# Layer 1's q, k and v by seven products of halves, in a two-layer graph kernel

## The chip, the cores and the metric

The kernel runs on one core of one Trainium2 chip. The core has TensorE (PE, matrix products; its weight loads are shown as PEld), VectorE (DVE), ScalarE (ACT), GpSimd (POOL) and SyncE (SP, which here issues nearly all DMAs). The metric is the device time of one execution in microseconds; less is better.

## The reference

`x` has 128 graphs of 128 nodes with 512 features, in float32; `adj` is a boolean 128x128 matrix for each graph. Two residual layers follow each other. Each one normalises `x` row by row, takes the positive part `h`, and adds an attention-like mix.

```python
# layer 0, 8 heads of 64
h   = relu(layernorm(x))
m   = h @ map_w.T + map_b;   n = m / |m| per head
q   = m @ q_w.T + q_b;       k = m @ k_w.T + k_b
p   = softmax(where(adj, -1e10, q k^T / 8)) * keep
a   = (n n^T > 0.1) * p
x   = x + relu((a @ sem) @ gcn_W.T / (sum(a) + 1))      # sem = h @ gcn_map_w.T + b
# layer 1, 4 heads of 64
h   = relu(layernorm(x))
q, k, v = h @ Wq, h @ Wk, h @ Wv                         # 512 -> 256 each
x   = x + softmax(where(adj, q k^T / 8, -inf)) @ v @ Wo + bo
```

All products are float32 products. Each float32 product appears in the profile as two records on TensorE.

## The kernel before, in words

**Blocks and turns.** Two graphs (`g` = 0, 1) make one block, so there are 64 blocks of 256 nodes. All work of a block is cut into named steps, which are methods of `Block`. The order of the steps is written out by hand in the list `TURN`: an entry `(back, step, ...)` means that in turn t the step is recorded for block t - back. A loop records the list turn by turn, and the engines run their own instructions strictly in that order. So one turn holds layer 0's projections of block t, layer 0's attention of block t - 1, its mix and layer 1's q, k and v of block t - 2, layer 1's attention of block t - 3, and its mix and output projection of block t - 4. Entries with a negative `back` prepare later blocks.

**Layer 0's projections by seven products.** `h` of a block (two graphs by two halves of the features) is a 2x2 arrangement of quarters A; the weights are a 2x2 arrangement of blocks. The four output quarters are computed with seven quarter products in place of eight, the scheme of Winograd. `halves` (L360) makes four sums S1 to S4 of the quarters of `h` on GpSimd. `sums_of_weights` (L172) makes four sums of the weight blocks, once. `p(kind, i)` (L377) is product i; products 1 and 2 go to bank X, 6, 7 and 4 to bank Y, 5 and 3 to bank Z. Between them, `r`, `u` and `c` read the banks at an intermediate state and add: `r` 1 copies X with a bias after product 1 and `r` 2 is the same with another bias; `u` 1 is Y + r after product 6, `u` 2 is Y + r after product 7; `c` writes an output quarter from a bank and one of these. As the next product adds to the same bank, it has to wait for the reader. This is done for two kinds: `qk` (query and key, weights stationary, 128-column records) and `ms` (m and sem, activations stationary, 512-column records).

**Layer 1's q, k and v.** They are plain products: `qk1` (L745) makes q and k with 8 matmuls each, weights stationary and both graphs' 256 nodes moving; `v1` (L768) has 8 matmuls with activations stationary and 256 weight columns moving. `qk1_out` and `v1_out` copy the results out of PSUM on ScalarE, q with a factor of 1/8.

**PSUM and buffers.** All eight PSUM banks are one rotating pool (`mm_bank`, L60): a new bank is the one given out eight requests before, and its first product waits for that one's last reader. SBUF pools `keep1`, `keep2`, `keep3`, `keep6` and `squares` (2 buffers) rotate in the same way.

**Transpositions.** Data that must be turned is transposed in 32x32 squares on VectorE, written to DRAM in four DMAs (`put`, L207), read back in one (`get`, L217), and joined by a ScalarE copy. This is done for layer 0's h (`h0`, `h0_put`, `h0_get`, `h0_out`), for n, for the thresholded attention (`near_T`, `near_put`, `near_get`, `near_T_out`), for layer 1's h (`h1` and so on) and for its attention (`attn_T`, `attn_put`, `attn_get`). Blocks at the start and end use TensorE for some of them.

**Layer 0's end.** `mix0` (L668) multiplies the turned attention by sem, `mix0_out` (L686) scales it into `x1`, `reload` loads x again as `xr` and `residual` (L708) adds it to `x1` on GpSimd; then `stats1`, `rstd`, `norm1`, `h1` follow.

Of the kernel before, what the change touches and what calls it, by code (L numbers as in the profile page):

```python
# [8 lines left out]
F32 = mybir.dt.float32  # L9
# [6 lines left out]
P = 128  # L16
# [4 lines left out]
def kernel(  # L21
# [51 lines left out]
    w_q1 = const.tile([P, KC, INNER], F32, name="w_q1")  # L73
    w_k1 = const.tile([P, KC, INNER], F32, name="w_k1")
    w_v1 = const.tile([P, KC, INNER], F32, name="w_v1")
# [95 lines left out]

    def sums_of_weights(w):  # L172
        nc.vector.tensor_sub(w[:, T3], w[:, B22], w[:, T1])
        nc.vector.tensor_sub(w[:, T1], w[:, T1], w[:, B11])
        nc.vector.tensor_sub(w[:, T2], w[:, B22], w[:, T1])
        nc.vector.tensor_sub(w[:, T4], w[:, B21], w[:, T2])
# [48 lines left out]
    class Block:  # L225
# [17 lines left out]
        def load_x(self, tag):  # L243
            b = self.b
            t = keep1.tile([P, G, D], F32, tag=tag, name=f"{tag}_{b}")
            nc.sync.dma_start(out=t, in_=x[b * G : (b + 1) * G].rearrange("g s d -> s g d"))
            return t


        def reload(self):  # L250
            self.xr = self.load_x("xr")
# [99 lines left out]
        def h0_out(self):  # L351
            self.hT = self.joined(("hn", 0), "hT", AF.Relu)
# [4 lines left out]
        def quarters(self):  # L357
            return [[self.hT[:, g, 2 * k : 2 * k + 2, :] for k in range(2)] for g in range(G)]

        def halves(self):  # L360
            A = self.quarters()
            t = keep1.tile([P, 4, 2, S], F32, tag="halves", name=f"halves_{self.b}")
            S1, S2, S3, S4 = (t[:, i] for i in range(4))
            nc.gpsimd.tensor_tensor(S1, A[1][0], A[1][1], ALU.add)  # L364
            nc.gpsimd.tensor_tensor(S2, S1, A[0][0], ALU.subtract)
            nc.gpsimd.tensor_tensor(S3, A[0][0], A[1][0], ALU.subtract)
            nc.gpsimd.tensor_tensor(S4, A[0][1], S2, ALU.subtract)
            self.f["S"] = (S1, S2, S3, S4)
# [8 lines left out]
        def p(self, kind, i):  # L377
            A = self.quarters()
            S = self.f.get("S")
# [10 lines left out]
            if kind == "ms":  # L390
                for c in range(2):
                    nc.tensor.matmul(  # L392
                        bank,
                        lhsT=src[:, c, :],
                        rhs=w_ms[:, w, c, :],
# [6 lines left out]
            for oc in range(KC):  # L402
                for c in range(2):
                    nc.tensor.matmul(  # L404
                        bank[:, oc * P : (oc + 1) * P],
                        lhsT=w_qk[:, w, c, oc * P : (oc + 1) * P],
# [6 lines left out]
        def sums(self, nm):  # L413
            pool = keep1 if nm == "r1" else keep2
            return pool.tile([P, D], F32, tag=nm, name=f"{nm}_{self.b}_{len(self.f)}")

        def r(self, kind, i):
            if i == 1:
                self.f[kind, "r1"] = r = self.sums("r1")
                if kind == "ms":  # L420
                    nc.vector.tensor_add(r, self.f[kind, "X"], b_ms[:, 1])
                    return
                for oc in range(KC):
                    cols = slice(oc * P, (oc + 1) * P)
                    nc.scalar.activation(
                        r[:, cols], self.f[kind, "X"][:, cols], AF.Identity, bias=b_k[:, oc : oc + 1]
                    )
                return
            self.f[kind, "r2"] = r = self.sums("r2")
            if kind == "ms":  # L430
                nc.gpsimd.tensor_tensor(r, self.f[kind, "r1"], b_d, ALU.add)
            else:
                nc.gpsimd.tensor_tensor(
                    r.rearrange("p (c t) -> p c t", t=S),
                    self.f[kind, "r1"].rearrange("p (c t) -> p c t", t=S),
# [4 lines left out]
        def u(self, kind, i):  # L440
            r = self.f[kind, "r1"]
            if i == 1:
                self.f[kind, "u1"] = self.sums("u1")
                nc.vector.tensor_add(self.f[kind, "u1"], self.f[kind, "Y"], r)  # L444
            else:
                nc.vector.tensor_add(r, self.f[kind, "Y"], r)  # L446

        def c(self, kind, g, half):
            bank, other = (("X", None), ("Z", "u1"), ("Y", "r2"), ("Z", "r1"))[2 * g + half]
            bank = self.f[kind, bank]  # L450
            if kind == "ms":
                other = b_ms[:, 0] if other is None else self.f[kind, other]
                hh = H0 // 2
                nc.vector.tensor_add(  # L454
                    mss[:, :: 1 + self.b % 2, g, half * hh : (half + 1) * hh, :DK][:, :2],
                    bank.rearrange("p (k h d) -> p k h d", k=2, d=DK),
                    other.rearrange("p (k h d) -> p k h d", k=2, d=DK),
                )
                return
            nm = ("qT", "kT")[half]  # L460
            if nm not in self.f:
                self.f[nm] = keep1.tile([P, KC, T], F32, tag=nm, name=f"{nm}_{self.b}")
            out = self.f[nm][:, :, self.cols(g)]
            if other is None:
                for oc in range(KC):
                    nc.scalar.activation(
                        out[:, oc],
                        bank[:, oc * P : (oc + 1) * P],
                        AF.Identity,
                        bias=b_q[:, oc : oc + 1],  # L470
                    )
            else:
                nc.vector.tensor_add(
                    out,
                    bank.rearrange("p (c t) -> p c t", t=S),
                    self.f[kind, other].rearrange("p (c t) -> p c t", t=S),
                )
# [208 lines left out]
        def mix0_out(self, g):  # L686
# [8 lines left out]
            if "x1" not in f:  # L695
                f["x1"] = self.x1 = keep3.tile([P, G, D], F32, tag="x1", name=f"x1_{b}")
            x1 = self.x1[:, g, :]
            for i in range(2):
                nc.vector.scalar_tensor_tensor(
                    x1.rearrange("p (i h d) -> p i h d", i=2, d=DK)[:, i],  # L700
# [7 lines left out]
        def residual(self, g):  # L708
            x1 = self.x1[:, g, :]
            nc.gpsimd.tensor_add(x1, x1, self.xr[:, g, :])  # L710
# [33 lines left out]

        def qk1(self, nm, w):  # L745
            pq = mm_bank(f"p{nm}_{self.b}").rearrange("p (c t) -> p c t", t=T)
            for oc in range(IC):
                for c in range(KC):
                    nc.tensor.matmul(  # L749
                        pq[:, oc, :],  # L750
                        lhsT=w[:, c, oc * P : (oc + 1) * P],
                        rhs=self.h1T[:, :, c, :],
                        start=(c == 0),
                        stop=(c == KC - 1),
                    )
            self.f["p", nm] = pq

        def qk1_out(self, nm):
            self.f[nm] = keep1.tile([P, IC, T], F32, tag=nm, name=f"{nm}_{self.b}")
            nc.scalar.mul(self.f[nm], self.f["p", nm], SCALE if nm == "q1" else 1.0)  # L760

        def q1(self):
            self.qk1("q1", w_q1)

        def k1(self):
            self.qk1("k1", w_k1)

        def v1(self):  # L768
            pv = mm_bank(f"pv1_{self.b}").rearrange("p (g o) -> p g o", g=G)
            for g in range(G):  # L770
                for c in range(KC):
                    nc.tensor.matmul(  # L772
                        pv[:, g, :],
# [417 lines left out]
```

## Time and profile before

| what | value |
|---|---|
| median of three runs | 3073.66 us (3071.89 to 3075.13) |
| profiled execution | 3074.49 us, its span 3072.70 us |
| granted TensorE clock, mean | 0.996 |
| one turn in the middle (1498.30 to 1544.76 us) | 46.46 us |
| busy in that turn: PE, PEld, DVE, ACT, POOL | 46.46, 35.91, 33.95, 22.96, 24.54 us |
| DMA in that turn | 0.59 of 16 engines, 172 GB/s |

A page of the profile gives the busy time of each engine with its share of the span; then the chain of work that ended last, followed back from the last instruction, at each step to what released it. A timeline row has a start and a length in us, engine, line, operation, out<-in and a count; brackets hold the idle time before it and what ended it. In the chain a row has start, length, engine, tile and line. Rows of equal instructions are merged, and the length of a merged row is from the first start to the last end, so that rows that follow each other without a gap can overlap a little.

### The profile page before, as it was taken

Reading aid. Unit: us, or ns where it says so; the run is one execution under the profiler, and the core shown is the slowest. Engines: PE = TensorE matmul, PEld = TensorE weight load, DVE = VectorE, ACT = ScalarE, POOL = GpSimd, SP = SyncE. Lnnn points to the kernel's source line nnn. Section 1 sums busy time; section 2 is a strip of 40 time slices with the busy share of each in tenths; the row PEclk is TensorE's granted clock in tenths of the full one; section 3 lists DMA queues with packets and bytes.
Section 4 is the critical chain, followed back from the end, with each engine's and each line's share of the span. In section 5 each row is a group of like instructions: output and inputs, shape, how many; then the busy total and the mean of one; then the engine's idle time right before and its main releaser. Section 6 shows DMA issues by size and latency. Waiting matters only on the chain.

```text
span 3072.7 us, 62082 instructions
## 1 busy us (share of the span) xinstructions
PE 3037.7 (99%) x23024; PEld 2337.5 (76%) x23024; DVE 2177.1 (71%) x3913; ACT 1481.6 (48%) x4573; POOL 1572.8 (51%) x2183
## 2 busy tenths in 40 slices
PE   8999999999999999999999999999999999999997
PEld 5777777777777787787777777777777777777875
DVE  3677777777777777777777777777777777777763
ACT  2454554454454554544544544544544544544543
POOL 1555456455455455455455555554564564554552
PEclk9999999999999999999999999999999999999998
DMA  5346656655655555655555556566566556556541
GB/s 162 116 144 180 186 147 179 183 156 173 182 163 172 169 177 166 172 173 172 165 175 178 159 177 182 153 178 187 148 179 184 152 176 183 160 173 174 164 131 62
DMA packets 304206, 507.97 MB, mean 165 GB/s; under 512 B 49184, under 2 KB 180512, under 8 KB 295968
## 3 DMA queue, kind: packets, MB, share of 16 engines
q1 hardware_dynamic: 301200, 503.44, 55.2%
q8 instruction: 182, 2.98, 0.4%
q10 hardware_dynamic: 2704, 0.57, 0.1%
q14 instruction: 120, 0.98, 0.1%
HBM read 273.72 MB, written 230.16 MB: 164 GB/s over the span
## 4 chain that ended last, share of the span: by engine, by line
PE 98%; DVE 1%; DMA 0%; ACT 0%; issue 0%; POOL 0%; ACTq 0%; SPq 0%; DVEq 0%; POOLq 0%
PE py_qk L404 11%; PE py_ms L392 11%; PE px_qk L404 8%; PE px_ms L392 8%; PE pz_qk L404 7%; PE pq L749 7%; PE pv L772 7%; PE pk L749 7%; PE pz_ms L392 7%; PE py L916 7%; PE po L676 4%; PE psc L541 4%; PE pc L541 4%; PE ps L541 2%; PE po L898 2%; PE pw_k L133 0%
## 5 line engine op out<-in xcount | busy, mean ns | idle before, releaser
L334 POOL TENSOR_SCALAR rstd<-mv 128x1 f32<-128x1 f32 x256 | 57.9, 226 | 886.1 <-DVE mv L198 875.6
L601 ACT ACTIVATE s<-s,mx 128x128 f32<-128x128 f32 x1024 | 396.4, 393 | 108.7 <-DVE mx L587 108.7
L481 ACT ACTIVATE n<-ms 128x512 f32<-128x512 f32 x128 | 80.3, 628 | 449.8 <-DVE ms L454 449.0
L838 ACT ACTIVATE s<-s,mx 128x128 f32<-128x128 f32 x512 | 199.2, 390 | 173.8 <-DVE mx L828 173.8
L404 PEld LDWEIGHTS py_qk<-halves,w_qk 128*128 128x128 f32 x2048 | 243.6, 192 | 28.7 <-POOL x L710 14.3
L404 PE MATMUL px_qk<-hT,w_qk 128*128 128x128 f32 x2048 | 256.0, 278 | 0.0
L404 PE MATMUL pz_qk<-halves,w_qk 128*128 128x128 f32 x2048 | 249.7, 275 | 0.0
L404 PE MATMUL py_qk<-halves,w_qk 128*128 128x128 f32 x2048 | 249.5, 275 | 0.0
L392 PE MATMUL px_ms<-w_ms,hT 128*128 128x512 f32 x512 | 247.2, 605 | 0.0
L404 PEld LDWEIGHTS px_qk<-hT,w_qk 128*128 128x128 f32 x2048 | 238.6, 192 | 7.6
L916 PE MATMUL py<-w_o,oT 128*128 128x512 f32 x512 | 242.6, 598 | 1.5 <-ACT oT L909 1.5
L392 PE MATMUL py_ms<-w_ms,halves 128*128 128x512 f32 x512 | 240.8, 593 | 1.6 <-DVE u L444 1.6
L392 PE MATMUL pz_ms<-w_ms,halves 128*128 128x512 f32 x512 | 240.6, 592 | 0.0
L404 PEld LDWEIGHTS pz_qk<-halves,w_qk 128*128 128x128 f32 x2048 | 239.0, 192 | 0.0
L749 PEld LDWEIGHTS pq<-h1T,w_q 128*128 128x128 f32 x1024 | 195.7, 191 | 56.8 <-issue 29.6
L749 PE MATMUL pq<-h1T,w_q 128*128 128x256 f32 x1024 | 233.4, 381 | 3.2 <-ACT h1T L739 3.2
L364 POOL TENSOR_TENSOR halves<-hT 128x256 f32<-128x256 f32 x64 | 47.2, 738 | 368.5 <-PE pz_ms L392 354.8
L772 PEld LDWEIGHTS pv<-w_v,h1T 128*128 128x128 f32 x1024 | 194.7, 190 | 52.7 <-issue 29.6
L446 DVE TENSOR_TENSOR r<-py_ms,r 128x512 f32<-128x512 f32 x64 | 44.3, 692 | 265.5 <-PE py_ms L392 265.5
L749 PE MATMUL pk<-h1T,w_k 128*128 128x256 f32 x1024 | 231.5, 379 | 0.0
L772 PE MATMUL pv<-w_v,h1T 128*128 128x256 f32 x1024 | 231.5, 379 | 0.0
L497 POOL TENSOR_TENSOR rn<-rn,mhalf 128x8 f32<-128x8 f32 x128 | 213.2, 1666 | 8.4 <-DVE rn L492 8.4
(130 smaller groups left out, 6766.4 us busy)
## 6 DMA issues: line engine op xcount, KB each, us to landing
d_h<-hn SPq DMA_DIRECT2D x504, 128.0 KB, 3.6
mv<-d_h SPq DMA_DIRECT2D x126, 512.0 KB, 4.4
d_near<-s SPq DMA_DIRECT2D x248, 256.0 KB, 4.0
near_mv<-d_near SPq DMA_DIRECT2D x62, 1024.0 KB, 5.6
xt<-in_x SPq DMA_DIRECT2D x64, 512.0 KB, 7.5
xr<-in_x SPq DMA_DIRECT2D x64, 512.0 KB, 6.6
out<-x SPq DMA_DIRECT2D x128, 256.0 KB, 5.7
d_attn<-s SPq DMA_DIRECT2D x252, 128.0 KB, 3.0
```

The lines of the kernel that those rows point to most:

```text
L392: nc.tensor.matmul(bank, lhsT=src[:, c, :], rhs=w_ms[:, w, c, :], start=(first and c == 0), stop=(c == 1), skip_group_check=True,)
L404: nc.tensor.matmul(bank[:, oc * P : (oc + 1) * P], lhsT=w_qk[:, w, c, oc * P : (oc + 1) * P], rhs=src[:, c, :], start=(first and c == 0 an ...
L481: nc.scalar.activation(n2.rearrange("p (h d) -> p h d", d=DK), mss[:, 0, g, :, :DK], AF.Square)
L497: nc.gpsimd.tensor_tensor(rn, rn, mhalf[:, :H0], ALU.pow)
L541: nc.tensor.matmul(dst[par][:, :, first + step * p, :], lhsT=lT(rows, p), rhs=rT(rows, p), start=True, stop=True,)
L601: nc.scalar.activation(s[:, :, g, par, c, :], s[:, :, g, par, c, :], AF.Exp, bias=mx[:, i : i + 1], accum_out=z[:, h : h + 1],)
L676: nc.tensor.matmul(po[h // PR][half * DK : (half + 1) * DK, h % PR, :], lhsT=f["nearT", g][:, (h % 2) * PR + h // 2, half * DK : (half + 1 ...
L749: nc.tensor.matmul(pq[:, oc, :], lhsT=w[:, c, oc * P : (oc + 1) * P], rhs=self.h1T[:, :, c, :], start=(c == 0), stop=(c == KC - 1),)
L772: nc.tensor.matmul(pv[:, g, :], lhsT=self.h1T[:, g, c, :], rhs=w_v1[:, c, :], start=(c == 0), stop=(c == KC - 1),)
L838: nc.scalar.activation(s[:, :, par, c, g, :], s[:, :, par, c, g, :], AF.Exp, bias=mx[:, par, c, g : g + 1], accum_out=z[:, par, c, g : g + 1],
L898: nc.tensor.matmul(po[par * DK : (par + 1) * DK, g, c, :], lhsT=self.f["v1"][:, g, h * DK : (h + 1) * DK], rhs=self.f["aT"][:, :, par, c, ...
L916: nc.tensor.matmul(py, lhsT=self.f["oT"][:, g, c, :], rhs=w_o1[:, c, :], start=(c == 0), stop=(c == IC - 1),)
```

## The change

Layer 1's q and k (as one product h @ [Wq | Wk]) and v get the seven-product scheme too, as kinds `qk1` and `v`. `halves(1)` makes the four sums of layer 1's h on GpSimd. The methods `p`, `r`, `u`, `c` serve all four kinds. `dest` gives the place of an output quarter, and sums are kept in it: `u` writes to the place of its quarter and `c` adds to that in place, so the tile `u1` is gone; for the new kinds `r` is a ScalarE copy into the place of quarter (0, 0), which later gets its final value. The factor 1/8 of q moves into the weights. `hT` has one buffer in place of two. `x1` is now the reloaded x; `mix0_out` writes to a tile `mix`, which `residual` adds to it.

The weights of layer 1 are loaded as blocks, and their two scalings and eight sums are recorded one by one behind `u` and `c` of `ms` in turns 0 and 1 (`one_piece`).

`TURN` is written anew. TensorE's order in a turn was: mix0 0, mix1, mix0 1, scores0 1 and 0, qk products 1, 6, 2, 5, 7, 4, 3 (with the two output projections after 1 and after 7), scores1, near 0 and 1, ms 1, 5, 6, q1, k1, ms 7, 2, 4, 3, v1. It becomes: mix0 0, mix1, mix0 1, scores0 0 and 1, qk 1, 6, projection, 2, 7, projection, 5, 4, 3, scores1, near 1 and 0, ms 1, 6, 5, qk1 1, ms 7, 2, 4, 3, qk1 6, v 1, 6, qk1 7, 2, 5, v 2, 7, qk1 4, 3, v 5, 4, 3. `unit` 1 and `nT` of a block move from the start of the next turn to the end of its own.

```diff
-    w_q1 = const.tile([P, KC, INNER], F32, name="w_q1")
-    w_k1 = const.tile([P, KC, INNER], F32, name="w_k1")
-    w_v1 = const.tile([P, KC, INNER], F32, name="w_v1")
+    w_qk1 = const.tile([P, 7, 2, INNER], F32, name="w_qk1")
+    w_v1 = const.tile([P, 7, 2, INNER // 2], F32, name="w_v1")
...
         def reload(self):
-            self.xr = self.load_x("xr")
+            self.x1 = self.load_x("x1", keep3)
...
-            if kind == "ms":
+            if kind in ("ms", "v"):
                 for c in range(2):
+                    rhs = (w_ms if kind == "ms" else w_v1)[:, w, c, :]
                     nc.tensor.matmul(
-                        bank,
+                        bank[:, : rhs.shape[1]],
                         lhsT=src[:, c, :],
-                        rhs=w_ms[:, w, c, :],
+                        rhs=rhs,
...
-            for oc in range(KC):
+            for oc in range(IC if layer else KC):
                 for c in range(2):
                     nc.tensor.matmul(
                         bank[:, oc * P : (oc + 1) * P],
-                        lhsT=w_qk[:, w, c, oc * P : (oc + 1) * P],
+                        lhsT=(w_qk1 if layer else w_qk)[:, w, c, oc * P : (oc + 1) * P],
                         rhs=src[:, c, :],
...
+        def dest(self, kind, g, half):
+            b, f = self.b, self.f
+            if kind == "ms":
+                hh = H0 // 2
+                return mss[:, :: 1 + b % 2, g, half * hh : (half + 1) * hh, :DK][:, :2]
+            if kind == "v":
+                if "v1" not in f:
+                    f["v1"] = keep2.tile([P, G, INNER], F32, tag="v1", name=f"v1_{b}")
+                return f["v1"][:, g, half * P : (half + 1) * P]
+            n = KC if kind == "qk" else IC
+            nm = (("qT", "kT") if kind == "qk" else ("q1", "k1"))[half]
+            if nm not in f:
+                f[nm] = keep1.tile([P, n, T], F32, tag=nm, name=f"{nm}_{b}")
+            return f[nm][:, :, self.cols(g)]
...
         def r(self, kind, i):
+            X = self.f[kind, "X"]
+            if kind in ("qk1", "v"):
+                self.f[kind, "r1"] = self.f[kind, "r2"] = r = self.dest(kind, 0, 0)
+                nc.scalar.copy(r, self.shaped(kind, X))
+                return
...
         def u(self, kind, i):
-            r = self.f[kind, "r1"]
-            if i == 1:
-                self.f[kind, "u1"] = self.sums("u1")
-                nc.vector.tensor_add(self.f[kind, "u1"], self.f[kind, "Y"], r)
-            else:
-                nc.vector.tensor_add(r, self.f[kind, "Y"], r)
+            Y = self.shaped(kind, self.f[kind, "Y"])
+            nc.vector.tensor_add(self.dest(kind, i - 1, 1), Y, self.f[kind, "r1"])
 
         def c(self, kind, g, half):
...
+            bank = self.shaped(kind, self.f[kind, ("XZ", "YZ")[g][half]])
+            out = self.dest(kind, g, half)
+            if half:
+                nc.vector.tensor_add(out, bank, out)
+            elif g:
+                nc.vector.tensor_add(out, bank, self.f[kind, "r2"])
+            elif kind == "ms":
+                nc.vector.tensor_add(out, bank, self.shaped(kind, b_ms[:, 0]))
...
             else:
-                nc.vector.tensor_add(
...
+                nc.scalar.copy(out, bank)
...
         def residual(self, g):
             x1 = self.x1[:, g, :]
-            nc.gpsimd.tensor_add(x1, x1, self.xr[:, g, :])
+            nc.gpsimd.tensor_add(x1, x1, self.f["mix", g])
...
+        later = [("scale", w_qk1, w) for w in (B11, B21)]
+        later += [("sub", w, *sum) for w in (w_qk1, w_v1) for sum in SUMS]
```

The last third of the new list, from `near`'s transpositions on:

```python
(3, "exps1", 0), (3, "exps1", 1), (1, "near_T", 1), (3, "weights1"), (1, "near_T", 0),
(0, "u", "ms", 2), (-2, "norm0", 1), (0, "c", "ms", 1, 1), (0, "p", "ms", 4), (2, "halves", 1),
(0, "c", "ms", 0, 0), (0, "r", "ms", 2), (3, "scale1"), (2, "r", "qk1", 1), (-2, "rstd", 0, 0),
(4, "store", 0), (0, "p", "ms", 3), (2, "p", "qk1", 6), (3, "attn_T"), (1, "near_put"),
(0, "c", "ms", 1, 0), (2, "masks1"), (-1, "h0_out"), (3, "attn_put"), (2, "p", "v", 1),
(0, "c", "ms", 0, 1), (-2, "norm0", 0), (2, "u", "qk1", 1), (0, "squares", 0), (1, "near_get"),
(3, "attn_get"), (2, "r", "v", 1), (0, "norms", 0), (2, "p", "v", 6), (2, "u", "v", 1),
(2, "p", "qk1", 7), (-2, "h0"), (0, "squares", 1), (2, "p", "qk1", 2), (2, "p", "qk1", 5),
(2, "u", "qk1", 2), (0, "unit", 0), (2, "c", "qk1", 1, 1), (2, "p", "v", 2), (0, "norms", 1),
(2, "p", "v", 7), (2, "p", "qk1", 4), (2, "u", "v", 2), (2, "p", "qk1", 3), (2, "p", "v", 5),
(0, "unit", 1), (2, "c", "qk1", 1, 0), (2, "c", "qk1", 0, 1), (-1, "halves", 0), (1, "reload"),
(2, "p", "v", 4), (2, "c", "v", 1, 1), (2, "c", "v", 1, 0), (2, "c", "qk1", 0, 0),
(1, "near_T_out", 0), (2, "c", "v", 0, 0), (2, "p", "v", 3), (0, "nT"), (2, "c", "v", 0, 1),
(-3, "load"), (-2, "h0_put"), (1, "near_T_out", 1),
```

## The prediction

> **What bounds the kernel now.** I read the busy shares and the chain of work first, then a window of the chain in the middle of the run, and then the other engines' instructions in that window. The first fence is from the profile page.
>
> ```profile
> PE 3037.7 (99%) x23024; PEld 2337.5 (76%) x23024; DVE 2177.1 (71%) x3913; ACT 1481.6 (48%) x4573; POOL 1572.8 (51%) x2183
> ...
> PE 98%; DVE 1%; DMA 0%; ACT 0%; issue 0%; POOL 0%; ACTq 0%; SPq 0%; DVEq 0%; POOLq 0%
> ```
>
> TensorE is 99% busy and makes up 98% of the chain. The chain in a window of one turn (start, length, what):
>
> ```profile
> 1501.19 1.99 PE psc L541 x32
> 1503.17 1.98 PE px_qk L404 x16
> 1505.15 1.72 PE py L916 x4
> 1506.87 1.78 PE py_qk L404 x16
> ...
> 1527.53 3.45 PE pq L749 x16
> 1530.98 3.45 PE pk L749 x16
> ...
> 1541.31 3.45 PE pv L772 x16
> 1544.76 1.09 PE po L676 x32
> ```
>
> Each piece starts where the last ended. The turn from 1498.30 to 1544.76 has 46.46 us of busy PE in 46.46 us of time, and the stretch 2000 to 2464.6 us has 464.60 in 464.60. So TensorE alone sets a turn, and its waits are in filling and draining: 35.0 us (3072.7 less 3037.7). VectorE has 33.95 of the 46.46 us, GpSimd 24.54, ScalarE 22.96.
>
> **The products.** A float32 product gives two records. A record of 128 columns takes 1.787/16 = 0.1117 us (py_qk; px_qk above also pays 0.19 for the change from 64-row tiles, as before and after), one of 256 columns 3.45/16 = 0.2158, half of which is 0.1079. Removed in a turn: q, k and v, 3 x 16 records, 3 x 3.45 = 10.35 us. Added: q and k together, seven products of 2 x 2 matmuls, 28, and v, seven of 2, 14; 42 x 2 = 84 records x 0.1117 = 9.38 us. TensorE is left with 45.49 us a turn, 0.97 less. The ideal eighth would be 1.29; the shorter records give 0.32 of it back. [...] Loads rise from 48 to 84 a turn. The busiest row here (py_qk on PEld, 243.6 us for 2048) is 119 ns a load: if that paced, 84 x 0.119 = 10.0 us, a gain of 0.35. But that row itself has a load for each 128-column record and runs at 0.1117; I take the row of the chain, 0.97.
>
> **The other engines.** VectorE gets ten more sums a turn: five of 128x256 (u twice, c three times, for qk1), like the 416 ns of the score sum of that size (L815), and five of 128x128 for v. These have no row; between nothing and 416, by the slope from 692 (128x512) to 416 I estimate 0.28. Sum 5 x 0.416 + 5 x 0.28 = 3.5 us, 37.4 of 45.5. ScalarE loses 0.597 + 0.597 + 0.575 and gets four copies, two like the 128x256 copy of L167 (375 ns) and two shorter: -1.0 to -0.3 us. GpSimd gets four half sums more, 0.738 + 3 x 0.73 = 2.9 us: 27.5 of 45.5. None becomes the bound by its sum, so these cost nothing while their order keeps them ahead of TensorE; if they were exposed they would cost their length. The residual adds into the loaded x (the same GpSimd sum, 1.27 us). Its 512 KB load still stands behind the attention's return on SP: issued about T 41.2 it lands 6.6 us later, T 2.3 of the next turn, and mix0_out 0, which the residual also needs, ends at T 3.5. The weights' sums are ten VectorE operations, six of 128x512 (0.69, as c) and four of 128x256 (0.416), 5.8 us, spread behind u and c of ms in turns 0 and 1; VectorE is busy 29.8 of the 46.5 us from 40.0 to 86.5, so they are hidden there; bounds 0 and 2 us in all, I take zero.
>
> **What may come too late.** I laid TensorE's new order out from the pieces' lengths, T = 0 at the first mix0, and put each producer's length behind what it needs. For example, product 2 of ms ends after mix0 1.09, mix1 0.87, mix0 0.94, scores0 1.99, product 1 of qk 1.98, six more of qk 10.73, two projections 3.44, scores1 1.09, near 1.79, product 1 of ms 1.91, four more of ms 6.88 and one of qk1 0.89: T 33.60. Then come products 4 and 3 of ms, to 37.04, and the other 13 of qk1 and v, to 45.49. What has room: h1T is there near T 22.9 and first used at 29.3, though its return now queues behind h0's on SP (512 KB, 4.4 us); halves1 end near 25.8, used at 37.0. The other moved things meet at two places.
>
> *First, the last product of v.* Product 5 of v ends at 44.61, VectorE's c v 1 1 takes 0.28 and ends at 44.93 after its handover of 0.04, and product 3, which adds to the same bank, is due at 45.05: only product 4 (0.447) covers it. What a just-missed wait costs is seen in the first turns:
>
> ```profile
> 56.89 1.81 PE py_qk L404 x16
> 58.79 0.70 DVE r L446
> 59.53 2.05 PE py_qk L404 x16
> 61.58 1.79 PE pz_qk L404 x16
> ```
>
> The group after the wait takes 2.05, not 1.79: a restart of 0.26 besides the wait. Bounds 0 and 0.26 a turn; I take 0.12, since the wait clears just before the group is due.
>
> *Second, the returns of near and attention.* SP runs in order: four puts of near, four of attn, then the two returns. The timelines of SP, then VectorE, then ScalarE in the turn above, and how long near's return takes to land:
>
> ```profile
> 1532.13 2.79 SPq L212 DMA_DIRECT2D d_attn<-s  x4
> 1535.28 0.34 SPq L219 DMA_DIRECT2D near_mv<-d_near  x1
> 1537.34 0.34 SPq L219 DMA_DIRECT2D aT<-d_attn  x1
> ```
> ```profile
> 1530.86 1.25 DVE L871 STREAM_TRANSPOSE s<-s 128x1024 f32<-128x1024 f32 x1 [0.80 <-POOL s L858]
> ```
> ```profile
> 1542.61 1.03 ACT L662 COPY s<-near_mv 128x1024 f32<-128x1024 f32 x1
> ```
> ```profile
> DMA to landing us min/median/max: 4.7/5.6/6.3
> ```
>
> The copy that mix0 needs ends at 1543.64, 1.1 us ahead of mix0 (1544.76). In the new order attn_T stands behind c ms 0 0 on VectorE, which waits for product 2 of ms, ended at T 33.60. From there: handover 0.04, c 0.61 (start to start), transposition 1.25, SP 0.08, first put to near's return 3.15, landing 5.5 (mean of 25 turns), handovers 0.10, copy 1.03 = 11.76; TensorE has 45.49 - 33.60 = 11.89 before it needs it. Room 0.13 us, less than the landing's spread. The attention's return is issued 2.05 later, lands in about 5.5 (up to 6.9) and is needed 1.09 later than near's: room 0.3. Bounds 0 and 0.5 us a turn (landing at the slow end, partly covered by the first stall); I take 0.15. Behind the late copy on ScalarE stand c v 0 0 and near_T_out 1, wanted at T 2.0; they would be ready at 1.1.
>
> A third place is nearer than it looks: nT now precedes c v 0 1 and mix0_out 0 on VectorE, and unit 1 (GpSimd, 1.68 + 1.19) precedes nT. From product 5 of qk1 (T 41.5): 0.40 + 0.95 + 2.9 + 1.25 + 0.28 + 1.65 = 48.9, and the bank that scores0 1 takes over is wanted at 49.4. Room 0.5; I count nothing.
>
> **The sum.** A turn loses 0.97 - 0.12 - 0.15 = 0.70 us. 62 turns of the 64 are covered by other work: 43.4 us. In the first turns five waits of the kind shown (three 7-then-4 of qk, two 6-then-7 of ms, 1.0 to 1.3 each, 5.5 us) get a product between them; I take 4.5. In the drain the last two blocks wait for halves1 (1.47 us to the second) with no other work: 1 us lost. 43.4 + 4.5 - 1 = 46.9. The profiled execution, 3074.49 (1.79 over its span), comes to 3027.6; the median shown is 0.83 below it: **3027 us**, 1.5% faster.
>
> **The rivals.** *All of it is kept* (rooms are larger than I laid them): 62 x 0.97 + 3.5 = 63.6, 3010 us. For it: every room is positive at the mean. Against: 0.13 us beside a landing spread of 1.6. *Most is lost*: the returns land 0.5 us later than now, or the weight loads pace (gain 0.35): 0.2 to 0.5 us a turn kept, 62 times that and 3.5: 3039 to 3058. For it: loads that rise from 48 to 84; against: the 0.1117 of a row with the same ratio. *Slower, by a wait that takes the place of the removed work*: mix0 waits for near's copy. It decides when the chain of 11.76 us passes 11.89 + 0.97 = 12.9, that is 1.1 us later than laid, for instance if the fourth put of attn stalls on SP (one of the turns after the one shown issues them in 3.83, not 2.79 us) and the landing is slow in most turns. At 13.5 us: 62 x 0.6 = 37 over before, 3111. Against: both at once were not in any turn I read. *No change*, TensorE's saving being eaten exactly, 3074, needs the same at 12.9.
>
> **How the numbers follow.** Part kept, the forecast (0.5 to 0.85 us a turn, 3018 to 3039): 0.42. All kept (3007 to 3018): 0.27. Most lost (3039 to 3067): 0.17. Within 0.2%, about what a measurement of this kernel can tell from no change (6 us): 0.04. Slower: 0.10. Range 3009 to 3053: outside lie about 0.02 of the second case, 0.04 of the third, and the last two, 0.14; together 0.20. Faster 0.86, same 0.04, slower 0.10.
>
> **What would show it.** Right: groups of qk1 of 8 records at 0.89 us and of v at 0.45; a turn of 45.5 to 46.0 us; a gap before the third product of v, or before mix0 with ScalarE's near copy or aT as releaser, of some tenths. Wrong: records of 128 columns over 0.1117 (weight loads pace); a wait of TensorE on VectorE at scores0; turns over 46.5 with mix0 or mix1 waiting.

## The result, and the profile after

The changed kernel takes 3035.83 us (median of four runs, 3033.84 to 3036.55) beside 3074.39 us for the kernel before on the same chip (3071.89 to 3075.41). The ratio is 0.9875, with a 95% interval of 0.9858 to 0.9892: 38.6 us or 1.25% faster. The forecast was 3027, its range 3009 to 3053. The profiled execution has a span of 3032.0 us, 40.7 less than before.

The busy shares on the page after:

```profile
PE 2990.2 (99%) x25328; PEld 2372.9 (78%) x25328; DVE 2410.0 (79%) x4563; ACT 1471.3 (49%) x4637; POOL 1768.7 (58%) x2439
```

TensorE has 2304 records more (36 in each of 64 blocks) and 47.5 us less to do. VectorE has risen by 233 us, 3.6 a block, and is still far from the bound. The chain of this page breaks off in the drain, so the turn is read from timelines. The products of layer 1 on TensorE in a turn in the middle (start, length from first start to last end, engine, line, what):

```profile
1517.49 1.06 PE L407 MATMUL px_qk<-h1T,w_qk 128*128 128x128 f32 x8
1518.38 1.06 PE L407 MATMUL pz_qk<-halves,w_qk 128*128 128x128 f32 x8
1519.27 0.61 PE L395 MATMUL px_v<-w_v,h1T 128*128 128x128 f32 x4
1519.72 0.61 PE L395 MATMUL py_v<-w_v,halves 128*128 128x128 f32 x4
...
1521.95 0.61 PE L395 MATMUL pz_v<-w_v,halves 128*128 128x128 f32 x4
1522.40 0.61 PE L395 MATMUL py_v<-w_v,h1T 128*128 128x128 f32 x4
1522.95 0.71 PE L395 MATMUL pz_v<-w_v,halves 128*128 128x128 f32 x4
1523.59 1.16 PE L692 MATMUL po<-ms,s 128*64 128x66 f32 x32
```

Read starts, not lengths: from one start to the next a product of q and k takes 0.89 us and one of v 0.45, as laid out (8 and 4 records of 0.1117). Apart from 0.03 us ahead of the first row, only around v's last product is there more: 0.55 before its start, and 0.64 before the heads' products (`po`, mix0), which take 0.54 there when the wait is gone (below). It waits for this sum on VectorE, which ends at 1522.89:

```profile
1522.60 0.29 DVE L482 TENSOR_TENSOR v<-pz_v,v 128x128 f32<-128x128 f32 x1
```

The first heads' products of a turn, in the kernel before (first two rows) and in the changed one, 60 turns apart:

```profile
197.06 1.16 PE L676 MATMUL po<-ms,s 128*64 128x66 f32 x32
2985.26 1.16 PE L676 MATMUL po<-ms,s 128*64 128x66 f32 x32
198.03 1.16 PE L692 MATMUL po<-ms,s 128*64 128x66 f32 x32
2940.56 1.16 PE L692 MATMUL po<-ms,s 128*64 128x66 f32 x32
```

That is 46.47 us a turn before and 45.71 now. So the turns gain 60 x 0.761 = 45.7 us; the start before them is 1.0 us later than before, and the rest after them is 91.4 us in place of 87.4, 4.0 more. That is the 40.7.

The return of near and attention, on SP, then ScalarE in the turn ahead of that one, whose heads' products start at 1477.88:

```profile
1467.72 1.78 SPq L211 DMA_DIRECT2D d_attn<-s  x4
1469.66 0.34 SPq L218 DMA_DIRECT2D near_mv<-d_near  x1
1472.14 0.34 SPq L218 DMA_DIRECT2D aT<-d_attn  x1
```
```profile
1476.01 0.37 ACT L493 COPY q<-px_qk 128x256 f32<-128x256 f32 x1 [3.99 <-DVE q L484]
1476.28 1.05 ACT L678 COPY s<-near_mv 128x1024 f32<-128x1024 f32 x1
```

Near lands 5.6 us after its issue, at 1475.3. Its copy starts only 1.0 us later, because it stands behind the copy of q's quarter (0, 0), which waits for a sum of VectorE; it ends at 1477.33, 0.55 us ahead of mix0, and no heads' product in the trace waits for it. So it is in 58 of the 60 turns; in the median, near has landed 1.2 us before its copy starts. The turn of the rows of layer 1 is one of the two others: its first put of attention is 2.89 us ahead of near's return, the longest of all (the median is 1.94), near lands at 1522.07, and the copy starts with the landing and ends 0.45 us ahead of mix0. The place behind q's copy is not in the prediction.

The fill. TensorE, GpSimd and VectorE in turn 2 (brackets: idle before, and what ended it):

```profile
111.55 2.06 PE L557 MATMUL psc<-kT,qT 64*128 64x128 f32 x32
117.09 2.94 PE L407 MATMUL px_qk<-hT,w_qk 128*128 128x128 f32 x16 [3.48 <-DVE mix L713]
119.82 2.71 PE L407 MATMUL py_qk<-halves,w_qk 128*128 128x128 f32 x16
122.36 1.95 PE L407 MATMUL px_qk<-hT,w_qk 128*128 128x128 f32 x16
```
```profile
113.40 1.19 POOL L523 TENSOR_TENSOR n<-ms,rn 128x256 f32<-128x256 f32 x2
114.62 1.25 DVE L305 STREAM_TRANSPOSE n<-n 128x1024 f32<-128x1024 f32 x1 [4.46 <-POOL n L523]
115.79 0.19 DVE L708 TENSOR_TENSOR r<-po,z 128x4 f32<-128x4 f32 x2
```

mix0_out, which frees TensorE's bank, stands behind nT on VectorE, and nT waits for unit 1 on GpSimd. In the steady turn above nT ends at 1524.98, 0.2 us behind mix0's products, and TensorE does not wait; in turn 2 unit 1 is done only at 114.6, 3 us behind them. TensorE loses 3.48 us, and the two groups behind it take 5.27 us where 3.58 is their pace. Between 50 and 198 us TensorE has three more waits over 0.3 us: 1.56 at 56.12 (product 7 of layer 0's q and k), 1.62 at 109.11 (the first heads' products) and 0.39 at 165.75. With the 3.48 that is 7.05 us; before there were six of 0.79 to 0.85, 4.98 us.

The drain. VectorE, then TensorE in the last turn but one:

```profile
2964.39 1.25 DVE L845 STREAM_TRANSPOSE s<-s 128x1024 f32<-128x1024 f32 x1 [2.15 <-POOL s L832]
2965.56 0.39 DVE L476 TENSOR_TENSOR k<-py_qk,q 128x256 f32<-128x256 f32 x1
```
```profile
2966.09 2.05 PE L407 MATMUL py_qk<-halves,w_qk 128*128 128x128 f32 x8 [3.44 <-DVE k L476]
2967.93 1.91 PE L407 MATMUL px_qk<-h1T,w_qk 128*128 128x128 f32 x8
2969.64 1.91 PE L407 MATMUL pz_qk<-halves,w_qk 128*128 128x128 f32 x8
```

The sum u of q and k stands behind attn_T, which waits for GpSimd; product 7 waits 3.44 us for it, and the three groups behind the wait run at half pace (5.26 us to the next group's start where 2.68 is their pace). The same is seen in the last turn (3.29 us at 2995.49). The drain as a whole loses less than these waits, since two of the kernel before got shorter in it (4.91 and 2.48 us at 3000.72 and 3032.00, where now 3.49 and 1.46 stand at 2954.60 and 2990.14).

### The profile page after: what moved, and what is told of

Its sections match the earlier page's. It is cut to its first block, busy times and chain, and to the rows that moved or that the text cites. A ratio compares the mean times of both kernels' runs of the same rounds, so it can differ in the third digit from the quotient of the medians.

```text
span 3032.0 us, 68538 instructions
## 1 busy us (share of the span) xinstructions
PE 2990.2 (99%) x25328; PEld 2372.9 (78%) x25328; DVE 2410.0 (79%) x4563; ACT 1471.3 (49%) x4637; POOL 1768.7 (58%) x2439
## 3 DMA queue, kind: packets, MB, share of 16 engines
q8 instruction: 201, 3.29, 0.4%
## 5 line engine op out<-in xcount | busy, mean ns | idle before, releaser
L407 PEld LDWEIGHTS py_qk<-halves,w_qk 128*128 128x128 f32 x3072 | 370.4, 193 | 41.4 <-issue 31.8
L407 PE MATMUL py_qk<-halves,w_qk 128*128 128x128 f32 x3072 | 389.2, 277 | 10.5 <-DVE k L476 6.7
L407 PEld LDWEIGHTS pz_qk<-halves,w_qk 128*128 128x128 f32 x3072 | 369.0, 192 | 28.7 <-issue 28.7
L407 PE MATMUL pz_qk<-halves,w_qk 128*128 128x128 f32 x3072 | 385.7, 275 | 0.0
L724 POOL TENSOR_TENSOR x<-x,mix 128x512 f32<-128x512 f32 x128 | 162.6, 1271 | 89.5 <-DVE mix L713 57.3
L617 ACT ACTIVATION_READ_ACCUMULATOR s<-s,mx 128x1 f32 x1024 | 196.6, 192 | 0.0
L395 PEld LDWEIGHTS pz_ms<-w_ms,halves 128*128 128x128 f32 x512 | 97.3, 190 | 122.5 <-issue 107.6
L832 POOL TENSOR_TENSOR s<-s,z 128x512 f32<-128x512 f32 x126 | 128.5, 1041 | 106.0 <-DVE z L822 106.0
L395 PEld LDWEIGHTS px_ms<-w_ms,hT 128*128 128x128 f32 x512 | 92.0, 189 | 99.5 <-issue 91.8
L641 DVE SCALAR_TENSOR_TENSOR s<-pc,s 128x512 f32<-128x512 f32 x256 | 163.6, 680 | 3.3 <-PE pc L557 3.1
```

Source lines behind the costliest of these rows:

```text
L395: nc.tensor.matmul(bank[:, : rhs.shape[1]], lhsT=src[:, c, :], rhs=rhs, start=(first and c == 0), stop=(c == 1), skip_group_check=True,)
L407: nc.tensor.matmul(bank[:, oc * P : (oc + 1) * P], lhsT=(w_qk1 if layer else w_qk)[:, w, c, oc * P : (oc + 1) * P], rhs=src[:, c, :], star ...
L617: nc.scalar.activation(s[:, :, g, par, c, :], s[:, :, g, par, c, :], AF.Exp, bias=mx[:, i : i + 1], accum_out=z[:, h : h + 1],)
L641: nc.vector.scalar_tensor_tensor(sp, cp, 0.1, sp, ALU.is_gt, ALU.mult,)
L724: nc.gpsimd.tensor_add(x1, x1, self.f["mix", g])
L832: nc.gpsimd.tensor_tensor(s[:, :, par].rearrange("p q c g j -> p q (c g) j"), s[:, :, par].rearrange("p q c g j -> p q (c g) j"), z[:, par ...
```

## The experiments

Three edits were tried on the changed kernel first, each against one of these places. The kernel before took 3074.57 us beside them, and 3075.05 to 3075.19 beside the later ones. The four or five times of one kernel lie 1 to 6 us apart, so a gain of 1 or 2 us between two medians is not clear of the noise by itself.

**v's fifth product earlier.** Product 5 of v and the sum that reads its bank move up, so that product 3 no longer follows closely.

```diff
         (2, "p", "v", 7),
+        (2, "p", "v", 5),
         (2, "p", "qk1", 4),
         (2, "u", "v", 2),
+        (2, "c", "v", 1, 1),
         (2, "p", "qk1", 3),
-        (2, "p", "v", 5),
...
-        (2, "c", "v", 1, 1),
```

> v's product 5 goes ahead of qk1's product 4, and its reader c v 1 1 with it, so that the last product of v finds its sum 1.3 us before it is due. Theory (a turn of the changed kernel has 45.49 us of products and 0.22 us at this one wait): the turn falls from 45.71 to about 45.5, 60 x 0.20 = 12 us, 3024. Rival (the 0.22 us are spread over the many short groups, as restarts or weight loads): the wait goes, the turn stays at 45.7, 3036.

Measured: 3032.13 us (ratio 0.9863, 0.9846 to 0.9879), a turn of 45.66. The theory's 3024 is missed: the wait of v's product is gone, but only 0.05 us of it is gained. The rival has the turn nearly right, but not the reason. TensorE, then what the heads' products waited for on ScalarE in the whole run (us, times):

```profile
1521.81 0.61 PE L395 MATMUL py_v<-w_v,h1T 128*128 128x128 f32 x4
1522.26 0.61 PE L395 MATMUL pz_v<-w_v,halves 128*128 128x128 f32 x4
1522.95 1.16 PE L692 MATMUL po<-ms,s 128*64 128x66 f32 x32
```
```profile
  ACT s L678: 17.0, 63
```

v's last product now starts 0.45 after its forerunner, and mix0 0.69 after that. In 63 turns the heads' products wait for near's copy (L678), 17.0 us in all by the records, nearly all of it at their weight loads; the products start 0.15 us later than without that wait. The changed kernel has no such entry. One wait took the place of the other: without v's wait TensorE comes early enough to meet the copy.

**The fill.** nT of turn 2 moves to just ahead of nT_put in that turn; in the steady turns it stays.

```diff
+        early.remove((0, "nT"))
+        second = list(TURN)
+        second.insert(second.index((1, "nT_put")), (1, "nT"))
```

> Only in turns 1 and 2: block 1's transposition of n goes behind mix0_out 0 of turn 2 on VectorE. Theory (the late start of the first full turn comes from nT, which waits for GpSimd's unit 1 and holds up mix0_out 0, whose bank TensorE wants): the 3.5 us wait at 117 us goes, with some of the slow records behind it, 3.5 to 5 us, 3031 to 3032. Rival (the weights' sums on VectorE in turns 0 and 1 are what fills those turns): no change, another wait takes its place.

Measured: 3034.31 us (0.9868, 0.9853 to 0.9883). The wait of 3.48 is gone, but of the 3.5 to 5 us the times show 1.5, which is within their spread. Others appear (1.27 us at 122.97, where VectorE is late from nT's new place on), and the first heads' products of the steady part come at 196.83, 1.2 us earlier than in the changed kernel. This start differs between executions, too: three other profiles with nT in its place (v's fifth product, the drain, near's copy alone) have it at 198.73 to 199.17, and two later ones with this edit (the three together, near's copy first) at 198.06 and 196.61. So the edit is worth some 1 to 2 us.

**The drain.** In the turns without new blocks attn_T and its put stand behind the sums u of q, k and v, and the two returns behind them.

```diff
+        drain = [t for t in TURN if t not in ((3, "attn_T"), (3, "attn_put"))]
+        at = drain.index((2, "u", "v", 1)) + 1
+        drain[at:at] = [(3, "attn_T"), (3, "attn_put")]
...
```

> Only in the turns after the last block has started: attn_T and attn_put go behind u qk1 1 and u v 1. Theory (4 of the missing us are in the drain, where qk1's product 7 waits 3.4 and 3.3 us for u behind attn_T, which waits for GpSimd's scale1): both waits fall to under 0.5 us, and 2 to 4 us are left of it at the end, since mix1 then waits for the attention's return, 3032 to 3034. Rival (the drain is bound by the attention chain itself, so that TensorE's wait only moves): no change, 3036.

Measured: 3030.95 us (0.9858, 0.9844 to 0.9873). From the last full turn to the end it is 88.2 us in place of 91.4. This is a little better than the theory's 3032, and clear of the noise: no run of either kernel lies among the other's. Product 7 waits no longer; what is late next is the attention's return, moved back with attn_T:

```profile
2975.81 1.09 PE L872 MATMUL po<-aT,v 128*64 128x128 f32 x16 [1.41 <-DMA aT<-d_attn]
...
2999.46 1.83 PE L872 MATMUL po<-aT,v 128*64 128x128 f32 x16 [2.87 <-DMA aT<-d_attn]
```

**The three together.**

> The three orders of e1_v5_first, e3_fill and e4_drain together. Theory: their gains add, 12 + 4 + 3 = 19 us, 3017. If the last product's wait is the only real one: 3024.

Measured: 3026.13 us (0.9842, 0.9828 to 0.9857), 9.7 less than the changed kernel, half of the theory's 19; the three alone gained 3.7, 1.5 and 4.9, so their gains add, but the first one's is not 12. The turn is still 45.66, with near's copy waited for.

**Near's copy first.** If that wait is only an order on ScalarE, it can be taken away there:

```diff
+        (1, "near_T_out", 0),
         (2, "c", "qk1", 0, 0),
-        (1, "near_T_out", 0),
```

> The three edits tried apart (v's fifth product earlier; nT of turn 2 moved; the drain's order) together, and in ScalarE's order near's first copy ahead of the copy of q's quarter (0, 0). Theory: with v's fifth product moved, the heads' products wait for near's copy (0.27 us per turn recorded on ScalarE), and the copy is late only because it stands behind the copy of q's quarter, which waits for a sum of VectorE; near itself has landed by then. With the copy ahead the heads' products start when TensorE reaches them: turn 45.66 to about 45.50, 3026 to about 3017 us (3014 to 3020). Rival: near's landing sets the copy; the turn stays at 45.66 and the time at 3026.

Measured: 3017.11 us (0.9816, 0.9803 to 0.9830), a turn of 45.51. This is the theory's number; the rival, that near's landing sets the copy, falls. ScalarE, then TensorE:

```profile
1513.40 1.05 ACT L678 COPY s<-near_mv 128x1024 f32<-128x1024 f32 x1 [2.68 <-DMA near_mv<-d_near]
1515.16 0.37 ACT L493 COPY q<-px_qk 128x256 f32<-128x256 f32 x1 [0.71 <-DVE q L484]
```
```profile
1515.85 0.61 PE L395 MATMUL pz_v<-w_v,halves 128*128 128x128 f32 x4
1516.39 1.16 PE L692 MATMUL po<-ms,s 128*64 128x66 f32 x32
```

The copy now starts when near lands and ends 1.9 us ahead of mix0, which follows v's last product by 0.54. The median of 60 turns is 1.4, and in the turn with the slowest landing only 0.07 is left, so this order has little to spare.

**The same edit alone** on the changed kernel:

> The changed kernel, and only near's first copy ahead of the copy of q's quarter on ScalarE. Theory: in the changed kernel the wait of v's last product ends last and near's copy has 0.45 us to spare, so this edit alone gains nothing: turn 45.71, 3034 to 3037 us. Rival: near's copy already sets part of the lost time: turn 45.6, 3029 us.

Measured: 3035.97 us (0.9874, 0.9860 to 0.9887), a turn of 45.71: nothing. So the 0.20 us a turn needs both edits: the first alone gives 0.05, the second alone 0, together 0.20.

**Near's return behind the attention's** on SP's queue, to measure the room that the prediction put at 0.13:

```diff
-        (1, "near_get"),
         (3, "attn_get"),
+        (1, "near_get"),
```

> The changed kernel with near's reload issued behind attention's on SyncE's queue, some 2.3 us later (1518.6 in place of 1516.3). By the prediction's chain (11.76 us of 11.89, a room of 0.13) the heads' products would come 2.1 us later in every turn, 3036 + 62 x 2.1 = 3166 us. By the trace of the changed kernel (near lands about 5.4 us after its issue, so at 1524.0, its copy ends at 1525.05, and the heads' products begin at 1523.59) it is 1.5 us, 3129 us (3110 to 3140). Below 3060: near's return has more room than either gives it.

Measured: 3140.71 us, 1.0217 times the kernel before (1.0201 to 1.0233), on average 1.69 us a turn more than the changed kernel, with near's copy as the releaser:

```profile
2907.11 1.16 PE L692 MATMUL po<-ms,s 128*64 128x66 f32 x32 [0.65 <-ACT s L678]
...
2954.47 1.16 PE L692 MATMUL po<-ms,s 128*64 128x66 f32 x32 [1.58 <-ACT s L678]
```

Both expectations miss, the second by under 1 us, and that is in part luck, since the turns are not alike. Where near lands in up to 5.7 us, about as in the changed kernel (27 turns of 59), a turn takes 46.47 in the median, 0.76 more than 45.71; in the other 32 near takes up to 7.7 us to land, and the median is 48.0. Why it lands late there stays open. As the return is issued 2.3 us later, the room for it in the changed kernel was 2.3 less 0.76, about 1.5 us, and not 0.13.

**No sums of layer 1's weights**, so that the output is another.

```diff
-        later += [("sub", w, *sum) for w in (w_qk1, w_v1) for sum in SUMS]
+        later = []
...
+        nc.gpsimd.memset(w_qk1[:, T2:], 0.01)
+        nc.gpsimd.memset(w_v1[:, T2:], 0.01)
```

> The changed kernel without the ten scalings and sums of layer 1's weights for each of the two tensors: GpSimd fills the blocks behind the second with a constant at the start, so the output is another; the turns are the same. Theory: these sums cost the fill little: within 1.5 us of the changed kernel (3034.3 to 3037). Rival: the fill lost its predicted gain to them: 3 to 5 us less, 3031 to 3033.

Measured: 3033.25 us (0.9865, 0.9852 to 0.9879), 2.6 less than the changed kernel, between the two expectations. The wait for mix0_out in turn 2 is there without the sums (2.30 us, then 1.48 for kT), and the first heads' products of the steady part start at 198.82, not earlier than 198.03. So the sums did not take the fill's gain. The turn is the same, and the time from the last full turn on is 1.8 us shorter, where no such sum stands; so the profile shows no cost of the sums, and by the times it is 2.6 us at most.

**A plain v again**, q and k by seven products; the 16 matmuls of 256 columns stand where product 1 of v stood.

```diff
-        (2, "p", "v", 1),
+        (2, "v1"),
...
-        (2, "c", "v", 0, 0),
-        (2, "p", "v", 3),
+        (2, "v1_out"),
```

> Layer 1's v as one plain product again (16 matmuls of 256 columns, one copy on ScalarE), q and k by seven products. Theory: v's part of the gain is 3.45 less 3.13 us of matmuls = 0.32, and it brought the wait of its last product, 0.20 and 0.03: the turn should be 45.71 + 0.32 - 0.23 = 45.80, 3035.8 + 6 = 3041 us (3038 to 3045). Rival: v's part is worth its whole 0.32 (the lost time is not v's): 45.71 + 0.32 = 46.03, 3055 us.

Measured: 3134.85 us (1.0198, 1.0184 to 1.0212), slower than the kernel before, a turn of 47.35. Both expectations are far off. TensorE, with no product of v left between the last product of q and k and the heads' products:

```profile
1528.44 1.16 PE L692 MATMUL po<-ms,s 128*64 128x66 f32 x32 [1.20 <-ACT s L678]
```

It is near's copy behind the copy of q's quarter again; by the order, its cover was the products 5, 4 and 3 of v. To see whether this is all, the same v with near's copy first and the better ends of the last kernel below:

> The best version so far (3013.7 us, turn 45.51) with layer 1's v as one plain product again; near's first copy stays ahead of the copy of q's quarter. Theory: the slow turn of the other kernel with a plain v (47.35) came only from near's copy standing behind the copy of q's quarter, with no products of v left between the last product of q and k and the heads' products to hide it; here the heads' products wait for nothing, the turn is 45.51 + 0.32 = 45.83, and the time 3013.7 + 62 x 0.32 = 3033.5 us (3030 to 3037). Rival: the plain v has a delay of its own in that place (its bank, its copy on ScalarE): the wait stays near 1.2 us and the time is above 3080.

Measured: 3127.88 us (1.0174, 1.0160 to 1.0188), a turn of 47.33. The theory fails: near's copy is waited for in 6 turns only, but the next thing stands behind it. VectorE, then TensorE:

```profile
1525.74 1.25 DVE L305 STREAM_TRANSPOSE n<-n 128x1024 f32<-128x1024 f32 x1 [2.04 <-POOL n L523]
```
```profile
1528.52 1.13 PE L557 MATMUL psc<-kT,qT 64*128 64x128 f32 x14 [1.07 <-DVE mix L713]
```

That is the prediction's third place: nT ahead of mix0_out 0 on VectorE, and scores0 1 wants the bank. Then the plain v at the end, where the kernel before had it:

> As the last kernel with a plain v, but its 16 matmuls stand behind the last product of q and k, ahead of the heads' products, where the kernel before had them (there they stood at 1519 of a turn whose heads' products begin at 1523, that is ahead of four products of q and k). Theory: a plain v costs 0.32 us more of TensorE and nothing else; the 1.5 us beyond it (a turn of 47.33) came because layer 1's last sums and nT had no product of v left to hide them. Here the turn is 45.51 + 0.32 = 45.83 and the time 3033.5 us (3030 to 3037). Rival: the plain v has a delay of its own wherever it stands: the turn stays above 46.5, the time above 3075.

Measured: 3091.96 us (1.0055, 1.0041 to 1.0068), a turn of 46.73; between the two again. The heads' products and scores0 wait for nothing, but product 7 of q and k, which now follows product 6 at once in the same bank, waits for the sum between them:

```profile
1495.50 1.05 PE L407 MATMUL py_qk<-halves,w_qk 128*128 128x128 f32 x8
...
1497.23 1.13 PE L407 MATMUL py_qk<-halves,w_qk 128*128 128x128 f32 x8 [0.68 <-DVE k L476]
```

1.73 us from start to start in place of 0.89: 0.84 lost. 46.73 less 0.84 is 45.89, 0.38 above 45.51, beside 0.32 expected for v's matmuls; so v's own part is seen only after taking that wait off, and no run has it alone. What the three runs show is another thing: v's short products lie between and behind those of q and k as cover. Without them each of the three kernels waits in another place, 0.7 to 1.2 us a turn as recorded, and its turn is 0.9 to 1.5 us longer than v's matmuls account for.

**The best version** has near's copy first, v's fifth product earlier, and for the ends, on top of the two edits above, nT of turn 2 with its put behind the residual of group 1, and attn_T of the drain behind the sum of q and k.

> As the one before, with two more changes at the ends alone: in turn 2 nT and its transfer stand behind mix0_out and residual of group 1 (in the steady turn they keep their places), and in the drain attn_T and its transfer stand behind the second sum of q and k, not behind that of v. Theory: the wait of 2.83 us in turn 2 shrinks to about 1.3 and the waits of mix1 for aT in the drain (0.77 and 2.99) to 0 and about 2: 2 to 3 us less than the one before, about 3014.5. Rival: other waits take their places, no difference (3017).

Measured: 3013.66 us (0.9801, 0.9788 to 0.9815), 22.2 us under the changed kernel. The theory's 3014.5 came true. The steady part begins at 195.06 (198.03 in the changed kernel) and the time behind it is 85.3 us (91.4).

## Why the prediction was right, and where it was not

| step | predicted | measured |
|---|---|---|
| a turn without late waits | 45.49 us | 45.51 (near's copy first) |
| v's last product | 0.12 a turn | 0.20 (45.71 less 45.51) |
| returns of near and attention | 0.15 a turn | 0 |
| a turn | 45.76 us | 45.71 |
| 60 turns | 42.0 gained (60 of the 62 x 0.70) | 45.7 gained |
| the first turns | 4.5 gained | 1.0 lost |
| the drain | 1 lost | 4.0 lost |
| all | 46.9 gained (with 1.4 for two more turns) | 40.7 (profiled spans) |

The likeliest case, part kept, came true, for the reason given: the shorter products are worth 0.96 us a turn (46.47 less 45.51), and a part is lost at waits. That the turn came within 0.05 us, and the time within 9 us, is in part luck. In the turn, 0.08 too little for v's last product and 0.15 too much for the returns nearly cancel; in the whole, the ends came out 9.9 us worse than forecast (5.0 lost, where 4.9 were to be gained with the two more turns), and the 60 turns 3.7 us better. The products were sized rightly: 84 records at 0.1117. The pace of 0.119 us a weight load, which would have left a gain of 0.35, is not seen: q and k keep 0.89 for eight records with eight loads, 0.111 each.

*v's last product* was found at the right place with its releaser, and undersized: it loses 0.10 before its start and about as much after it, 0.20 of the bounds of 0 to 0.26. The upper bound was itself misread. The 2.05 us of the group in the prediction's rows is its whole length; by starts, the next group of the kernel before follows after 1.89:

```profile
59.53 2.05 PE L404 MATMUL py_qk<-hT,w_qk 128*128 128x128 f32 x16 [0.85 <-DVE r L446]
61.42 1.95 PE L404 MATMUL pz_qk<-halves,w_qk 128*128 128x128 f32 x16
```

So the restart was 0.10 us there, as it is at v's last product; the other 0.10 is the wait itself, which the prediction's layout had as just cleared.

*The returns* were charged 0.15 and cost nothing. The mis-sized term is the stretch from the first put to near's return: 1.94 us in the median turn, not 3.15. Near landed in 5.5 as said, and v's wait gave 0.2 more; so the room was some 1.6 us, not 0.13 (0.4 in the tightest of the 60 turns), which agrees with the 1.5 from near's late return. The two late things are not independent either: a wait ahead of mix0 gives its time to the copy, so their losses do not add when they stand in series. The tight place on ScalarE was another, the copy of q's quarter that near's copy is queued behind. The prediction named what is behind near's copy, and not what is ahead of it. Because of it, taking v's wait away is worth 0.05 until the order on ScalarE is changed.

*The first turns and the drain* hold the miss. The gain of 4.5 looked only at waits that the change removes. Those of 0.79 to 0.85 did get covered, but the same new order put nT ahead of mix0_out on VectorE, and in turn 2, where unit 1 is not early, this costs 3.48 us and the slow groups behind it 1.7, together 5.2. That is the prediction's third place; the steady turn was examined for it, the first turns were not. The waits of 1.56 and 1.62 are new as well. In the drain halves1 were charged with 1.47 us and took 1.46, but u behind attn_T was not looked at: 3.44 and 3.29 us, and 2.6 and 1.7 of half pace behind them. The drain's order alone returned 4.9 us, the fill's 1.5, and the refined ends together 3.5 more. Both ends vary between executions: the five profiles that have the changed kernel's drain take 89.7 to 92.3 us from the last full turn on, so the 4.0 and the 1.0 are good to a microsecond or two.

The slower rival, mix0 waiting for near's copy, was not reached in the changed kernel; near's return 2.3 us later on the queue brings exactly it, 1.69 a turn on average. The rest did as said: the weights' sums cost nothing that the trace shows and at most 2.6 us by the times (the bound was 2), VectorE's sums took 0.42 (128x256) and 0.25 to 0.29 us (128x128), and no engine became the bound.

## What to carry to other kernels

When an engine is full, list for each of its waits what stands ahead of the releaser in its own queue, not only what the releaser needs; the second late thing in that list decides what removing the first is worth, and only both edits together may show a gain (here 0.05 and 0 us a turn apart, 0.20 together). Lay the first and the last turns out by themselves: an order that is free in the steady turn can put a step behind one that is late only there (3.48 us in turn 2). Short independent products between dependent ones are cover, and a change that makes them shorter or moves them is to be costed as cover too (with a plain v a turn was 0.9 to 1.5 us longer than v's matmuls account for).

## What was not expected of the hardware

Behind some waits TensorE goes on at half pace for a while, here for 5.4 us behind a wait of 3.44 us. The drain of the changed kernel by stretches (length, busy us and instructions of PE, PEld, DVE, ACT and POOL, granted clock, DMA share, GB/s):

```profile
2966.00:2968.00 2.00, 1.91 (x9) 1.94 (x10) 0.14 (x1) 0.00 (x0) 0.00 (x0) 0.50 0.66 148
2968.00:2970.00 2.00, 2.00 (x11) 2.00 (x11) 0.42 (x1) 0.00 (x0) 0.00 (x0) 0.50 0.40 114
2970.00:2972.00 2.00, 2.00 (x14) 2.00 (x12) 0.41 (x1) 0.00 (x0) 0.00 (x0) 0.62 0.76 246
2972.00:2974.00 2.00, 2.00 (x20) 2.00 (x19) 0.73 (x3) 0.06 (x1) 0.00 (x0) 1.00 0.79 205
```

The granted clock is 0.50 for 5.4 us behind the wait of 3.44 us, and 2.6 us are lost there, so that wait costs 6.0 us in all; behind the one of 1.46 us it stays at 1.00. In the drain without the waits of product 7 it is 0.50 from 2999.7 to 3006.5 us, behind the wait of 2.87 us for the attention. It is seen behind a shorter wait, too. This is the kernel with nT of turn 2 moved, behind the wait of 1.62 us for the first heads' products:

```profile
112.00:115.00 3.00, 3.00 (x40) 2.88 (x38) 1.42 (x4) 0.00 (x0) 2.92 (x5) 0.50 0.52 130
```

This wait, of 1.61 or 1.62 us, stands in the changed kernel and in eight of its edits: nT of turn 2, the drain, the three together, near's copy first, the best version, no sums, a plain v, and a plain v at the end. From its end the heads' products and scores0 take 4.5 us in three of the nine (the changed kernel, the three together, the best version) and 6.0 to 6.1 us in the other six; in the changed kernel the fall comes behind the wait of 3.48 us. With near's return late, mix1 and mix0 1 behind a wait of 2.83 us (at 2811.27) take 1.66 and 1.88 us from start to start; behind waits of 2.00 and 2.26 us (at 2860.68 and 1485.48) they take 0.87 and 1.04, 0.88 and 1.03. So the length of the wait alone does not tell whether the clock falls, and what does is not shown here. The stretches at 0.50 in the changed kernel are 3.4 or 6.8 us long, but for the one that runs into the end. A wait in the fill or the drain is to be costed with what may come behind it: here 1.5 to 2.6 us, behind waits of 1.62 to 3.48 us.
